# A hybrid transformer block on one core: two output heads projected together in the second feed-forward, its layernorm's last pass on ScalarE, and the first layernorms two tiles ahead

## The chip, the core and the metric

The kernel runs on one core of one Trainium2 chip. A core has a matrix engine (TensorE, "PE" in the profile, with its weight loads shown apart as "PEld"), a vector engine (VectorE, "DVE"), an engine for activations (ScalarE, "ACT"), a general engine (GpSimd, "POOL") and a synchronizing engine (SyncE, "SP"), which here only issues transfers. Each engine works through its own instructions in order; semaphores make one engine wait for another. Data lies in SBUF, 128 partitions wide; matrix products land in PSUM.

The metric is the device time of one execution in microseconds. Before the change it is 1683.34 us in the median of three runs (1683.14 to 1686.43).

## What is computed

The reference is a block of four residual stages over T = 1024 tokens of C = 512 channels, all in fp32:

```python
x = x + attn_a(layernorm(x), wq, wk, wv, wo)          # 32 heads of 16 channels, causal, rotary
x = x + ffn(layernorm(x), W_base, b_base, W_router, lora_A, lora_B)
x = x + attn_b(layernorm(x), Wq, Wk, Wv, Wo, ...)     # 32 heads of 128, 8 groups of keys and values, alibi
x = x + ffn(layernorm(x), W_base, b_base, W_router, lora_A, lora_B)

def layernorm(x):
    m = mean(x); v = var(x)
    return (x - m) / sqrt(v + eps)

def ffn(x, W_base, b_base, W_router, lora_A, lora_B): # the top 2 of 8 experts, rank 16 each
    w = top2_weights(softmax(x @ W_router.T))
    h = einsum('td,erd->ter', x, lora_A)
    return x @ W_base.T + b_base + 2.0 * einsum('ter,eor,te->to', h, lora_B, w)
```

The output of attn_b is the concatenation of its 32 heads times Wo, so it is a sum over heads: each head's 128 channels are multiplied with their own 128 rows of Wo. Which heads are summed in PSUM and which are added to x in SBUF is free, but for rounding.

## The kernel before

**Tiles.** x stays in SBUF in fp32 as NT = 8 tiles, x[0] to x[7], of 128 tokens by 512 channels. TensorE contracts over partitions, so a normalized tile is transposed first: `channels` (L118) makes four 128x128 transposes into PSUM (`transpose4`, L99; tiles tp_...) and copies them back with ScalarE (L121).

**The order of work.** A scheduler places each instruction on its engine by the order in which the program issues it, with some freedom by what is ready; the first layernorms' statistics are pinned to program order (`in_order`). From then on each engine's order is fixed. Pools of buffers (`bufs=`) set when a buffer may be written again.

**Layernorm.** `normalized` (L102 to L116) has bn_stats (L106), its aggregation (L110), the addition of eps (L112), all on VectorE, then the power -1/2 on GpSimd (`rsqrt`, L93: a tensor_tensor with a tile of -0.5, tile rs), then the last pass (L115) on VectorE: (x - mean) * rs, 128x512.

**Attention a, projections.** `project_qk` (inside `project_a`, from L202) runs over the tiles. In turn i it issues the four products of q for tile i (L179), the layernorm of tile i + 1, then `rotate` for q (L185 on ScalarE, L189 and L190 on VectorE), the transposes of tile i + 1 (`columns`, tiles tp_a), then the products of k and their rotation, and then what turn i - 1 left to be turned into rows (tp_aq, tp_ak). From the second half on, attention's own steps stand between these turns; among them are maxima over score tiles (L319, L322) on VectorE. The normalized tiles xn_a share the tag "w" (4 buffers) with ScalarE's outputs in `rotate`. The tiles of x are loaded by SyncE; weights are loaded by ScalarE's and SyncE's queues, and from the middle of attention a on by GpSimd.

**Attention b.** It works in 8 groups g of four query heads (hh = 0 to 3). For each head and tile i, `softmax` (L785 to L803) issues the score products (L791, tiles s), on VectorE the scaling with the alibi bias (L793), the maximum (L797) and its negation with the slope (L798), on ScalarE the exponential with its sum (L800), on VectorE the reciprocal (L802), on GpSimd the scaling (L803). Two tiles later `finish` issues the transposes of the probabilities by VectorE (L818, L824) and, at the end of a head (in the last group at its half too), the products with the values (L835; tiles o, and or for the rest), copied or added into oT, one for each head (L860, L876).

Between these steps TensorE is given other work as filler: `fill` is a generator that issues one matmul at each `next`. `due` says how many units of it are to be issued after the n-th tile of a group. Into the filler go the next group's projections and `project_o` (L636 to L648): for each tile t it multiplies oT of several heads with their rows of Wo into one PSUM tile (L642, tiles wo) and then adds it to x[t] on VectorE (L647). In the last group, g = 7, there is no next group. There the filler is the former group's projection (32 units), then heads 0 and 1 together (16 units: two matmuls and one addition for each tile), then head 2 alone (8 units: one matmul and one addition for each tile). Head 3 alone (8 more) is returned to the caller as `rest`, and runs in the second feed-forward. A tile's name has the group, the first head and the tile: wo7_2_4 is head 2's (and whatever is summed with it) product for tile 4. The wo tiles of the attention loop take turns in two PSUM buffers, those of the feed-forward in four.

**Feed-forward.** `ffn` (from L504) runs over NT + lag + 1 turns. In turn i it takes one turn of `before` (in the second feed-forward: the units of `rest`), `rows(i)` (the layernorm of tile i, xn_f with four buffers, then x[i] += bias on GpSimd, L525, which must come behind the last reading of x by the layernorm), `router(i - lag - 1)` (products with the router's and the experts' first weights, L534, tiles pr_f, copied by ScalarE, L535), `back(i - NT)` (products with W_base, L599, and with the second expert weights, added to x, L601) and `columns(i - lag)` (tp_f). After each four tiles comes `route`: a row of some thirty short VectorE instructions (L555 to L584) that picks two experts and ends in g_f; TensorE then transposes g_f (tp_g_f). The lag is 1 in the first feed-forward, f1, and 2 in the second, f2. Feed-forward f1 takes attention a's last output projections as its `before`; f2 ends with the transfers of the output, by SyncE.

Of the kernel before, what the change touches and what calls it, by code (L numbers as in the profile page):

```python
# [9 lines left out]
F32 = mybir.dt.float32  # L10
BF16 = mybir.dt.bfloat16
AF = mybir.ActivationFunctionType
ALU = mybir.AluOpType
# [3 lines left out]
P = 128  # L17
T = 1024
NT = T // P
C = 512  # L20
# [15 lines left out]
HKV = 8  # L36
GRP = HB // HKV
# [27 lines left out]
class Block:  # L65
# [33 lines left out]
            self.nc.tensor.transpose(ps[:, j, :], s, self.ident)  # L99
        return ps  # L100

    def normalized(self, i, xn, name, in_order=False):  # L102

        nc, sm = self.nc, self.sm
        st = sm.tile([P, 6], F32, tag="ln_st", name=f"st_{name}{i}")
        stats = nc.vector.bn_stats(st, self.x[i])  # L106
        if in_order:
            self.tc.keep_in_program_order(stats)
        mv = sm.tile([P, 2], F32, tag="ln_mv", name=f"mv_{name}{i}")
        nc.vector.bn_aggr(mv, st)  # L110
        ve = sm.tile([P, 1], F32, tag="ln_ve", name=f"ve_{name}{i}")
        nc.vector.tensor_scalar_add(ve, mv[:, 1:2], LN_EPS)  # L112
        rs = sm.tile([P, 1], F32, tag="ln_rs", name=f"rs_{name}{i}")
        self.rsqrt(rs, ve, [1])
        nc.vector.tensor_scalar(xn, self.x[i], mv[:, 0:1], rs, ALU.subtract, ALU.mult)  # L115
        return xn  # L116

    def channels(self, xn, dst, tp, name, tag="tp"):  # L118
# [31 lines left out]
    def project_a(self, ap, pt, work, ps_s, xnTs, qT, kT, v_p, wqT, wkT, wvT, rot):  # L150

        nc = self.nc

        w = {}

        def load(n, src, queue):
            w[n] = pt.tile([P, KC, C], F32, tag="p", name=f"w{n}")
            queue.dma_start(w[n], src.rearrange("(k p) n -> p k n", p=P))

        load("q", wqT, nc.scalar)  # L160
        rt = ap.tile([P, 4, NT], F32, tag="rot", name="rot_sb")
        nc.sync.dma_start(rt, rot)
        load("k", wkT, nc.sync)
        for i in range(2, NT):
            self.load_x(i)
        load("v", wvT, nc.sync)
        for n in range(6):
            self.transpose4(ps_s, [self.ident] * 4, f"i{n}", tag="s")
        rows = {}
        for n, fill in (("q", 0.0), ("k", 1.0)):  # L170
            t = pt.tile([P, 2, HA, PADA], F32, tag="p", name=f"r{n}")
            nc.gpsimd.memset(t[:, :, :, DA : DA + 1], fill)
            nc.gpsimd.memset(t[:, :, :, DA + 1 : PADA], 0.0)
            rows[n] = [t[:, a] for a in range(2)]

        def project(i, n):
            ps = ps_s.tile([P, C], F32, tag="s", name=f"pj_{n}{i}")
            for kc in range(KC):
                nc.tensor.matmul(ps, lhsT=xnTs[i][:, kc, :], rhs=w[n][:, kc, :], start=(kc == 0), stop=(kc == KC - 1))  # L179
            return ps  # L180

        def rotate(i, n, r, ps):
            cos, sin = rt[:, r, i : i + 1], rt[:, r + 1, i : i + 1]
            xs = work.tile([P, C], F32, tag="w", name=f"xs_{n}{i}")
            nc.scalar.activation(xs, ps, AF.Copy, scale=sin)  # L185
            pv = ps.rearrange("p (h d two) -> p h d two", d=DA // 2, two=2)
            sv = xs.rearrange("p (h d two) -> p h d two", d=DA // 2, two=2)
            dv = rows[n][i % 2][:, :, :DA].rearrange("p h (d two) -> p h d two", two=2)
            nc.vector.scalar_tensor_tensor(dv[:, :, :, 0], pv[:, :, :, 0], cos, sv[:, :, :, 1], ALU.mult, ALU.subtract)  # L189
            nc.vector.scalar_tensor_tensor(dv[:, :, :, 1], pv[:, :, :, 1], cos, sv[:, :, :, 0], ALU.mult, ALU.add)  # L190

        def to_rows(i, n, dst):

            for c0 in range(0, NCA, 4):
                src = [rows[n][i % 2][:, (c0 + c) * 4 : (c0 + c + 1) * 4, :].rearrange("p h d -> p (h d)") for c in range(4)]
                ps = self.transpose4(ps_s, src, f"a{n}{i}_{c0}", tag="s")
                copy = nc.scalar.copy if c0 else nc.vector.tensor_copy
                copy(dst[:, c0 : c0 + 4, i * P : (i + 1) * P], ps)

        pending = []  # L200

        def project_qk():  # L202
            def layernorm(i):
                return self.normalized(i, work.tile([P, C], F32, tag="w", name=f"xn_a{i}"), "a", in_order=True)

            def columns(i, xn):
                self.channels(xn, xnTs[i], ps_s, f"a{i}", tag="s")

            columns(0, layernorm(0))
            for i in range(NT):  # L210
                ps = project(i, "q")
                xn = layernorm(i + 1) if i + 1 < NT else None
                rotate(i, "q", 2, ps)
                if i + 1 < NT:
                    columns(i + 1, xn)
                rotate(i, "k", 0, project(i, "k"))
                while pending:
                    to_rows(*pending.pop(0))
                pending.extend([(i, "q", qT), (i, "k", kT)])
                yield  # L220

        def project_v():
            for i in range(NT):
                ps = project(i, "v")
                while pending:
                    to_rows(*pending.pop(0))
                nc.scalar.copy(v_p[:, i, :HA, :DA], ps.rearrange("p (h d) -> p h d", d=DA))
                yield

        return project_qk(), project_v()  # L230
# [273 lines left out]
    def ffn(self, name, before, after, lag):  # L504
# [4 lines left out]
        nc, tc, w = self.nc, self.tc, self.ffn_w  # L509
        H = NT // 2  # L510
        with ExitStack() as ctx:
            work = ctx.enter_context(tc.tile_pool(name=f"{name}_w", bufs=4))
# [4 lines left out]
            ps_m = ctx.enter_context(tc.tile_pool(name=f"{name}_pm", bufs=4, space=PSUM))  # L517
            xns, xnTs, lrs, gs, gTs = {}, {}, {}, {}, {}
# [1 line left out]
                lrs[half] = rp.tile([P, H, E + ER], F32, tag="lr", name=f"lr_{name}{half}")  # L520

            def rows(i):
                xns[i] = self.normalized(i, work.tile([P, C], F32, tag="xn", name=f"xn_{name}{i}"), name)

                nc.gpsimd.tensor_tensor(self.x[i], self.x[i], w["b"], ALU.add)  # L525

# [96 lines left out]
    def attention_b(self, ctx, wo_pool, WqT, WkT, WvT, WoT, qw, kw, xnT, missing, ffn_weights):  # L623
# [4 lines left out]
        nc, tc, sm = self.nc, self.tc, self.sm  # L628
# [5 lines left out]
        work = ctx.enter_context(tc.tile_pool(name="b_x", bufs=2))  # L634
# [15 lines left out]
        with ExitStack() as ctx:  # L650
# [227 lines left out]
            def in_turn(*gens):  # L878
                for g in gens:
                    yield from g  # L880
# [26 lines left out]
            for g in range(HKV):  # L907


                last = g == HKV - 1  # L910
                parts = []
                if not last:
                    wq, wkv = load_qkv(g + 1)
                    parts.append(project_kv(g + 1, wkv))
                    parts.append(project_q(g + 1, wq))
                if g:
                    parts.insert(-1, project_o(g - 1, wo, heads, ps_m, "m"))
                fill = in_turn(*parts)
                units = 74 if g else 42
                done = 0  # L920
                for hh in range(GRP):
                    if g and hh == 2:
                        if last:
                            for _ in fill:
                                pass
                        wo = load_o(g)
                        if last:
                            fill = in_turn(project_o(g, wo, [0, 1], ps_m, "m"), project_o(g, wo, [2], ps_m, "m"))
                    for i in range(NT):
                        p = softmax(g, hh, i)  # L930
                        n = hh * NT + i + 1
                        if not last:
                            due = units * n // (GRP * NT)
                        elif hh < 2:
                            due = max(0, (n - 2) * 32 // 14)
                        else:
                            due = 32 + max(0, 2 * (n - 19)) if n < 27 else 48 + (n - 27)
                        while done < due:
                            next(fill, None)
                            done += 1  # L940
                        pending.append((g, hh, i, p))
                        if len(pending) > LAG:
                            finish(*pending.pop(0))
                    if last and hh == GRP - 1:
                        for item in pending:
                            next(fill, None)
                            finish(*item)
                for _ in fill:
                    pass
                if g == HKV - 2:  # L950

                    self.load_ffn(wp, nc.sync, ("wkv", "wq"), *ffn_weights)
        return lambda ps_m: project_o(HKV - 1, wo, [GRP - 1], ps_m, "pm")


@with_exitstack
# [152 lines left out]
```

## Time and profile before

The profiled execution took 1683.11 us, of which the traced span is 1681.3 us. The page's first part gives each engine's busy time; the kernel's largest groups by TensorE are the score products of attention b (L791, 294.8 us), its query projections (L745, 246.2), and its output projection (L642, 241.8 us in 512 records: a product of 128x512 in fp32 appears as two records).

| quantity | value |
|---|---|
| median of the runs | 1683.34 us |
| profiled execution | 1683.11 us |
| its span | 1681.3 us |
| granted TensorE clock | 1.00 in every stretch looked at |
| L647 on VectorE, addition of a projected tile to x | 80 times, mean 677 ns |
| L115 on VectorE, last pass of the layernorm, xn_f | 16 times, mean 668 ns, median 546, longest 1561 |
| L93 on GpSimd, power for one tile's layernorm, rs_f | 16 times, mean 557 ns |
| L525 on GpSimd, addition of the bias to x | 16 times, mean 1306 ns |
| L121 on ScalarE, copy of a transposed tile, xnT_f | 16 times, mean 585 ns |

How to read such a page: busy times are summed over the span; a wait is an engine's idle time just before an instruction, with the instruction on another engine whose end released it. Idle time of an engine that is not the bottleneck costs nothing. A wait for several things is put down to what came last.

### The profile page before, as it was taken

Reading aid. Unit: us, or ns where it says so; the run is one execution under the profiler, and the core shown is the slowest. Engines: PE = TensorE matmul, PEld = TensorE weight load, DVE = VectorE, ACT = ScalarE, POOL = GpSimd, SP = SyncE. Lnnn points to the kernel's source line nnn. Section 1 sums busy time; section 2 is a strip of 40 time slices with the busy share of each in tenths; the row PEclk is TensorE's granted clock in tenths of the full one; section 3 lists DMA queues with packets and bytes.
Section 4 is the critical chain, followed back from the end, with each engine's and each line's share of the span. In section 5 each row is a group of like instructions: output and inputs, shape, how many; then the busy total and the mean of one; then the engine's idle time right before and its main releaser. Section 6 shows DMA issues by size and latency. Waiting matters only on the chain.

```text
span 1681.3 us, 32166 instructions
## 1 busy us (share of the span) xinstructions
PE 1652.6 (98%) x13016; PEld 940.7 (56%) x13016; DVE 1103.0 (66%) x2856; ACT 542.1 (32%) x1217; POOL 347.8 (21%) x508
## 2 busy tenths in 40 slices
PE   9999999999999999999999999999999999999988
PEld 5544444344555667556655665756655665566654
DVE  3556666662653886776677667676677766776773
ACT  2315555555111332233233223223223322322220
POOL 2000000000312332222123212222222321221140
PEclk9999999999999999999999999999999999999999
DMA  5000000001003201100200200110020020000001
GB/s 195 1 1 2 2 2 2 2 2 38 2 24 88 65 2 41 49 26 26 64 26 26 61 30 1 51 38 26 26 64 26 26 71 26 1 27 27 2 1 50
DMA packets 60868, 52.06 MB, mean 31 GB/s; under 512 B 5744, under 2 KB 47472, under 8 KB 60720
## 3 DMA queue, kind: packets, MB, share of 16 engines
q1 hardware_dynamic: 59408, 46.06, 9.2%
q0 software_dynamic: 784, 2.90, 0.4%
q8 instruction: 102, 1.67, 0.4%
q10 hardware_dynamic: 528, 1.05, 0.2%
q14 instruction: 46, 0.38, 0.1%
HBM read 30.98 MB, written 2.10 MB: 20 GB/s over the span
## 4 chain that ended last, share of the span: by engine, by line
PE 87%; DVE 10%; ACT 1%; POOL 1%; issue 1%; DVEq 0%; ACTq 0%; POOLq 0%
PE o L835 13%; PE pq L745 12%; PE s L791 12%; PE wo L642 9%; PE sT L354 7%; PE kv L700 7%; PE oT L389 5%; PE s L302 4%; PE pm_f L599 3%; PE or L835 3%; DVE p L793 3%; DVE nm L797 2%; DVE pT L818 2%; PE pj_v L179 2%; PE pm_ao L993 2%; PE pj_k L179 2%
## 5 line engine op out<-in xcount | busy, mean ns | idle before, releaser
L803 POOL TENSOR_SCALAR p<-p,rs 128x128 f32<-128x128 f32 (+7 forms) x256 | 190.8, 747 | 750.6 <-DVE rs L802 685.7
L800 ACT ACTIVATE p<-p,nm 128x128 f32<-128x128 f32 (+7 forms) x256 | 198.1, 774 | 453.4 <-DVE nm L798 443.0
L793 DVE SCALAR_TENSOR_TENSOR p<-s,rq,rel 128x512 f32<-128x512 f32 (+3 forms) x384 | 227.1, 605 | 119.4 <-PE s L791 118.8
L791 PE MATMUL s<-kT,qT 128*128 128x512 f32 (+3 forms) x768 | 294.8, 492 | 1.8 <-DVE p L793 1.5
L745 PE MATMUL pq<-xnTb,wq 128*128 128x512 f32 x512 | 246.2, 599 | 0.0
L642 PE MATMUL wo<-wo,oT 128*128 128x512 f32 x512 | 241.8, 594 | 3.4 <-DVE x L647 1.9
L791 PEld LDWEIGHTS s<-kT,qT 128*128 128x128 f32 x768 | 141.2, 190 | 165.8 <-issue 126.1
L835 PEld LDWEIGHTS o<-pT,va 32*128 32x128 f32 x5632 | 215.7, 185 | 28.5 <-DVE rs L802 11.8
L835 PE MATMUL o<-pT,va 32*128 32x128 f32 (+7 forms) x5632 | 224.6, 313 | 0.8
L818 DVE STREAM_TRANSPOSE pT<-p 128x640 f32<-128x640 f32 (+4 forms) x256 | 172.1, 673 | 73.1 <-PE o L835 54.7
L374 ACT ACTIVATE p<-sT 128x512 f32<-128x512 f32 (+1 forms) x320 | 157.5, 555 | 113.4 <-PE sT L372 70.9
L797 DVE TENSOR_REDUCE nm<-p 128x1 f32<-128x128 f32 (+7 forms) x256 | 188.2, 736 | 3.6
L302 PE MATMUL s<-kT,qT 32*128 32x512 f32 (+3 forms) x768 | 181.9, 522 | 0.0
L354 PE MATMUL sT<-qT,kT 32*128 32x512 f32 (+3 forms) x768 | 155.7, 521 | 0.0
L642 PEld LDWEIGHTS wo<-wo,oT 128*128 128x128 f32 x512 | 93.8, 190 | 87.5 <-issue 72.4
L745 PEld LDWEIGHTS pq<-xnTb,wq 128*128 128x128 f32 x512 | 92.3, 190 | 87.9 <-issue 80.2
L700 PE MATMUL kv<-wkv,xnTb 128*128 128x256 f32 x512 | 116.7, 382 | 4.4 <-DVE nm L798 4.0
L700 PEld LDWEIGHTS kv<-wkv,xnTb 128*128 128x128 f32 x512 | 95.8, 190 | 26.2 <-DVE nm L798 6.9
L319 DVE TENSOR_REDUCE part<-s 128x1 f32<-128x512 f32 x128 | 80.8, 684 | 40.6 <-PE s L302 36.0
L354 PEld LDWEIGHTS sT<-qT,kT 32*128 32x128 f32 x768 | 60.5, 183 | 62.2 <-issue 24.0
L860 ACT COPY oT<-o 128x1024 f32<-128x1024 f32 (+1 forms) x36 | 33.0, 916 | 181.8 <-PE o L835 176.6
L302 PEld LDWEIGHTS s<-kT,qT 32*128 32x128 f32 x768 | 76.4, 183 | 25.7 <-ACT p L374 10.3
(153 smaller groups left out, 1610.4 us busy)
## 6 DMA issues: line engine op xcount, KB each, us to landing
va<-v SPq DMA_DIRECT2D x256, 64.0 KB
wq<-in_b_WqT_dram SPq DMA_DIRECT2D x8, 1024.0 KB
wo<-in_b_WoT_dram SPq DMA_DIRECT2D x8, 1024.0 KB
x<-in_x_dram SPq DMA_DIRECT2D x8, 256.0 KB
wkv<-in_b_WkT_dram SPq DMA_DIRECT2D x8, 256.0 KB
wkv<-in_b_WvT_dram SPq DMA_DIRECT2D x8, 256.0 KB
out_dram<-x SPq DMA_DIRECT2D x8, 256.0 KB
wq<-in_a_wqT_dram ACTq DMA_DIRECT2D x1, 1024.0 KB
```

The source lines that it names most:

```text
L302: nc.tensor.matmul(made[j][:, at:end], lhsT=qT[rows_of(j), c, i * P : (i + 1) * P], rhs=kT[rows_of(j), c, kc * QC : kc * QC + end - at], s ...
L354: nc.tensor.matmul(made[j][:, at:end], lhsT=kT[rows_of(j), c, b * P : (b + 1) * P], rhs=qT[rows_of(j), c, (qc + 1) * QC - (end - at) : (qc ...
L642: nc.tensor.matmul(ps, lhsT=oTs[g, h][:, t * P : (t + 1) * P], rhs=wo[:, h, :], start=(h == heads[0]), stop=(h == heads[-1]))
L700: nc.tensor.matmul(ps.rearrange("p a b -> p (a b)"), lhsT=xnT[:, kc, i * P : (i + 1) * P], rhs=wkv[:, kc].rearrange("p a b -> p (a b)"), s ...
L745: nc.tensor.matmul(ps, lhsT=wq[:, kc, hh * DB : (hh + 1) * DB], rhs=xnT[:, kc, cols], start=(kc == 0), stop=(kc == KC - 1))
L791: nc.tensor.matmul(s, lhsT=qT[:, i * P : (i + 1) * P], rhs=kT[:, lo:hi], start=True, stop=True)
L793: nc.vector.scalar_tensor_tensor(p[:, lo:hi], s, rq[:, i : i + 1], rel[:, at + lo : at + hi], ALU.mult, ALU.add)
L797: nc.vector.tensor_reduce(nm, p[:, :w], AX.X, ALU.max, negate=True)
L800: nc.scalar.activation(p[:, :w], p[:, :w], AF.Exp, bias=nm, scale=slope, accum_out=ss)
L803: nc.gpsimd.tensor_scalar(p[:, :w], p[:, :w], rs, 1.0, ALU.mult, ALU.mult)
L818: nc.vector.transpose(PT[:, i : i + (NT - 1) * (m - 1) + 1 : NT - 1, :], p[:, : m * P].rearrange("p (j k) -> p j k", k=P))
L835: nc.tensor.matmul(cols(o[:, a], j), lhsT=vs[g][rows, j * NB + b, :], rhs=moving(j, rows, slice(b * B, (b + 1) * B)), start=(j == js[0] an ...
```

## The change

The change has three parts.

1. In `project_qk`, the layernorm of tile 1 is issued ahead of the loop, and turn i issues the layernorm of tile i + 2 instead of i + 1. The normalized tiles get a tag of their own with three buffers.
2. `normalized` gets a switch `scalar`, which the feed-forwards (both of them, as they share the code) set. With it, GpSimd computes mb = -(mean * rs) for the tile, 128x1, and ScalarE makes the last pass as Identity(rs * x + mb), in place of VectorE's subtract and multiply.
3. In the last group of attention b only heads 0 and 1 are projected in the attention loop, by a different `due`. Heads 2 and 3 are projected together in the second feed-forward, two matmuls and one addition for each tile, in place of one matmul and one addition there and one of each in the attention loop.

```diff
@@ normalized
-    def normalized(self, i, xn, name, in_order=False):
+    def normalized(self, i, xn, name, in_order=False, scalar=False):
...
         self.rsqrt(rs, ve, [1])
-        nc.vector.tensor_scalar(xn, self.x[i], mv[:, 0:1], rs, ALU.subtract, ALU.mult)
+        if scalar:
+            mb = sm.tile([P, 1], F32, tag="ln_mb", name=f"mb_{name}{i}")
+            nc.gpsimd.tensor_scalar(mb, mv[:, 0:1], rs, -1.0, ALU.mult, ALU.mult)
+            nc.scalar.activation(xn, self.x[i], AF.Identity, bias=mb, scale=rs)
+        else:
+            nc.vector.tensor_scalar(xn, self.x[i], mv[:, 0:1], rs, ALU.subtract, ALU.mult)
         return xn
@@ project_qk
             def layernorm(i):
-                return self.normalized(i, work.tile([P, C], F32, tag="w", name=f"xn_a{i}"), "a", in_order=True)
+                return self.normalized(i, work.tile([P, C], F32, tag="xn", name=f"xn_a{i}", bufs=3), "a", in_order=True)
...
             columns(0, layernorm(0))
+            xn = layernorm(1)
             for i in range(NT):
                 ps = project(i, "q")
-                xn = layernorm(i + 1) if i + 1 < NT else None
+                nxt = layernorm(i + 2) if i + 2 < NT else None
                 rotate(i, "q", 2, ps)
                 if i + 1 < NT:
                     columns(i + 1, xn)
+                xn = nxt
                 rotate(i, "k", 0, project(i, "k"))
@@ ffn, rows
-                xns[i] = self.normalized(i, work.tile([P, C], F32, tag="xn", name=f"xn_{name}{i}"), name)
+                xns[i] = self.normalized(i, work.tile([P, C], F32, tag="xn", name=f"xn_{name}{i}"), name, scalar=True)
@@ attention_b
                         if last:
-                            fill = in_turn(project_o(g, wo, [0, 1], ps_m, "m"), project_o(g, wo, [2], ps_m, "m"))
+                            fill = project_o(g, wo, heads[:2], ps_m, "m")
...
                         else:
-                            due = 32 + max(0, 2 * (n - 19)) if n < 27 else 48 + (n - 27)
+                            due = 32 + max(0, 16 * (n - 19) // 13)
...
-        return lambda ps_m: project_o(HKV - 1, wo, [GRP - 1], ps_m, "pm")
+
+        def remaining(ps_m):
+            units = project_o(HKV - 1, wo, heads[2:], ps_m, "pm")
+            for _ in range(NT):
+                for _ in heads[2:]:
+                    next(units)
+                yield
+
+        return remaining
```

## The prediction

> **What bounds the kernel now.** I read the page first (busy shares, the chain that ended last), then TensorE's waits, then busy time by stretch, then the timelines of the two stretches in which TensorE waits.
>
> ```profile
> span 1681.3 us, 32166 instructions
> ...
> PE 1652.6 (98%) x13016; PEld 940.7 (56%) x13016; DVE 1103.0 (66%) x2856; ACT 542.1 (32%) x1217; POOL 347.8 (21%) x508
> ...
> PE 87%; DVE 10%; ACT 1%; POOL 1%; issue 1%; DVEq 0%; ACTq 0%; POOLq 0%
> ```
>
> TensorE is busy for all but 1681.3 - 1652.6 = 28.7 us, and the change removes no matmul. So it can gain only out of these 28.7 us. Who owns them (line and tile, releaser, total, times, longest):
>
> ```profile
> PE kv L700 <- DVE nm L798: 4.0, 5, 0.8
> PE wo L642 <- DVE x L647: 1.9, 2, 1.3
> PE tp_a L99 <- DVE xn_a L115: 1.8, 2, 1.4
> PE tp_g_f L99 <- DVE g_f L584: 1.8, 1, 1.8
> PE pr_f L534 <- ACT xnT_f L121: 1.7, 1, 1.7
> PE tp_f L99 <- DVE xn_f L115: 1.7, 1, 1.7
> ```
>
> All but the first are places that the diff touches. By stretch (length, then busy time of PE, PEld, DVE, ACT, POOL): the first feed-forward, the end of attention_b, and the second feed-forward up to its first tp_g:
>
> ```profile
> 418.00:490.00 72.00, 70.84 (x273) 39.70 (x272) 44.45 (x130) 9.81 (x23) 19.16 (x26) 1.00 0.02 6
> ...
> 1557.00:1620.30 63.30, 59.81 (x867) 37.80 (x863) 47.84 (x103) 13.49 (x28) 11.42 (x15) 1.00 0.01 2
> 1620.30:1642.20 21.90, 16.71 (x94) 11.31 (x91) 18.40 (x53) 5.17 (x13) 13.23 (x13) 1.00 0.00 0
> ```
>
> TensorE idles 1.2, 3.5 and 5.2 us there, and DVE is busy for 84% of the last one. From tp_g at 1642.21 on, it works nearly without a gap. The granted clock is 1.00 throughout.
>
> **First layernorms two tiles ahead.** TensorE's two waits here:
>
> ```profile
> 19.41 0.66 PE L99 MATMUL tp_a<-ident,xn_a 128*128 128x128 f32 x4 [0.49 <-DVE xn_a L115]
> ...
> 67.53 0.63 PE L99 MATMUL tp_a<-ident,xn_a 128*128 128x128 f32 x4 [1.35 <-DVE xn_a L115]
> ```
>
> The second arises because four maxima of L322 (62.56 to 65.09) stand ahead of the seventh tile's layernorm on DVE. A tile earlier, that layernorm stands before them. Nothing is added: the same eight layernorms, with three buffers of their own; the bn_stats order is pinned. The risk is a new wait: the layernorm now stands a tile earlier than its x may have landed, ahead of rotate on DVE, with its pow ahead of DMA issues on POOL (10 to 13.5 us). Tile 2's bn_stats ran at 17.04 with no DMA wait; were x there only then, rotate's DVE part would end near 21.3, and tp_aq, its user, starts after 22.9. No transfer is moved on SP's queue. Bounds: -1.84 if both go, +0.5 if tile 2's x lands late. I take **-1.8**, since both waits have the row as their only releaser.
>
> **ScalarE's last pass.** Per tile and feed-forward it removes one DVE pass (xn_f, 546 ns undisturbed) and adds a 128x1 POOL multiply (mb) and a 128x512 Identity on ACT. Neither is in the trace. For ACT, the same shape with a bias pointer (L800) takes 719 ns, with a scale pointer (L185) 688. *ScalarE: Activation LUTs*, "What ACT_TABLE_LOAD costs", gives 186 ns + 0.833 per element + 93 per pointer operand: 186 + 427 + 2 x 93 = 0.80 us with two pointers; I take the row, 0.72, and keep 0.80. That page's "Rules for kernel authors" speaks against the edit: add and multiply belong on VectorE. By undisturbed rows it is right: 0.72 against 0.55. But beside POOL's L525 the DVE pass stretches (max 1561 ns), and DVE, not ACT (5.2 of 21.9 us busy), is crowded. For mb: POOL's tensor_scalar is 374 ns at 128 columns, 693 at 512, so a line through both gives 0.27 at one column; the 128x1 pow (L93) at 0.557 is the other end. I take 0.3.
>
> In the first feed-forward, xn_f is ready some 2 us before TensorE wants it (430.35 against 433.53), at the tightest tile 1 us (453.01 against 454.03); a path longer by 0.3 + 0.2 stays under this. The one wait there, 0.9 us, has the residual x as its other input. **0**, bounds -0.1 and +0.5 (the cover gone on one tile).
>
> **Heads 2 and 3 together.** Removed: eight adds at L647. Moved: head 2's eight matmuls (two records of 0.43, so 0.86 us each, 6.9 in all). Before, eight stand in the attention loop as fill; in the changed program's order, six fewer wo matmuls stand ahead of or_3, attention's last product (21 instead of 27), and eleven instead of five behind it. So TensorE's work up to or_3 shrinks by 6 x 0.86 = 5.2 us. Whether or_3 comes that much sooner depends on DVE's softmax chain, which ends there:
>
> ```profile
> 1601.87 1.09 DVE L797 TENSOR_REDUCE nm<-p 128x1 f32<-128x896 f32 x1
> 1602.87 0.68 DVE L647 TENSOR_TENSOR x<-x,wo 128x512 f32<-128x512 f32 x1
> 1603.47 0.15 DVE L798 TENSOR_SCALAR nm<-nm 128x1 f32<-128x1 f32 x1
> 1603.53 1.40 DVE L793 SCALAR_TENSOR_TENSOR p<-s,rq,rel 128x512 f32<-128x512 f32 x2
> 1604.88 0.16 DVE L802 RECIPROCAL rs<-ss 128x1 f32<-128x1 f32 x1
> 1604.96 0.67 DVE L647 TENSOR_TENSOR x<-x,wo 128x512 f32<-128x512 f32 x1
> 1605.54 1.21 DVE L797 TENSOR_REDUCE nm<-p 128x1 f32<-128x1024 f32 x1
> ```
>
> The adds sit between a maximum and its negation, so each delays the chain by its spacing of 0.60. In this stretch (1590 to 1610) eight stand; the changed order leaves four: 2.4 us off the chain. The last scores also come 5.2 us sooner, as six fill matmuls fewer stand ahead of them. Replayed by hand with the durations above, TensorE's waits before or_3 sum to about what they are now (0.3 to 0.7 before scores and product; 2.2 at wo_2_0, which takes the PSUM buffer that the add of tile 7 frees, where 1.3 was paid for wo_3_0; behind it stand three more wo and then the last product, which waits for DVE's chain anyway). **or_3 ends 5.2 us sooner**; bounds 2.4 (the adds alone) and 6.9 (all moved matmuls).
>
> Behind or_3, TensorE has 6 x 0.86 = 5.2 us more, of which 1.7 is met by two base matmuls (L599) that now stand behind tp_g instead of ahead of it. Per tile it has 2 x 0.86 (wo) + 0.93 (pr) + 0.44 (tp) = 3.09 us. The tile's feed through POOL, in order, is pow 0.55, mb 0.3, ACT's pass 0.72 (POOL's bias add L525 waits for it), L525 1.27, and gaps of some 0.25: 3.1 us. So POOL just keeps pace, and its idle in front of TensorE shrinks from 5.2 to about 1.3: 0.4 at pr of tile 5, 0.9 at tp_g, where DVE's 20 short instructions of route still stand. What waits behind ACT's Identity is xnT's copy (L121) and lr's (L535), 0.6 and 0.27 us, both short of their users. After tp_g all as before.
>
> So per term: end moves by (idle behind or_3) - (idle before, 5.2) + 5.2 of work - (lead of or_3), the base matmuls cancelling: 1.3 - 5.2 + 5.2 - 5.2 = **-3.9**. Sum: -1.8 + 0 - 3.9 = -5.7; I take 0.2 back for POOL's narrow margin: -5.5. The profiled execution took 1683.11 (span 1681.3 and 1.8 around it), the median is 1683.34: 1677.6 by the former, **1677.9** by the latter.
>
> **Rivals.** With I for the idle behind or_3 and L for its lead, each case is I - L - 1.84.
> A, the tail is a wash: the wait at wo_2_0 and those for scores grow to eat the fill that left, so L = 2.4, and I = 2.4: -1.8, **1681.5**. For it: the waits of this stretch are already there with the fill (3.5 us). Against: the scores themselves come sooner.
> B, all fits: I = 0, L = 6: -7.8, **1675.5**. Against: wo_2_0's wait and tp_g's are in the order.
> C, slower: POOL becomes the second feed-forward's bound. It serves pow, mb, then stands until ACT has passed, then adds; mb at 0.557, ACT at 0.80, and L525 drawn out beside DVE give 0.557 + 0.557 + 0.80 + 1.45 + 0.3 = 3.7 a tile, and ACT's pass held behind a copy that waits for TensorE adds 0.5: 4.2, which is 1.1 over TensorE's 3.09; six tiles of it make I = 6.6 + 0.9 = 7.5, and with L = 2.4 the change costs 7.5 - 2.4 - 1.84 = +3.3: **1686.6**. It decides from I = L + 1.84 on. For it: GpSimd's row is 13.2 busy of 21.9 us before mb is added, and *GPSIMD Engine Reference*, "1. Specifications", says that GpSimd shares its SBUF interfaces with VectorE. The trace agrees: L561 took 1.06 us beside L525, 0.19 elsewhere. At 0.19 for each such row the cost is nothing, at 1.06 some 0.9 on route's path. Against: the change takes DVE's passes and adds out of just this stretch.
> That the change doesn't do what it says is excluded by the order of instructions for heads and passes.
>
> **How the numbers follow.** Forecast (L 4 to 6, I 0.8 to 2.5) 0.62; A 0.18; B 0.09; C 0.11. The range, 1675.0 to 1682.8, holds forecast, B and most of A, and leaves C and the edges out; the likeliest alone is 1676.5 to 1680. About what a measurement can tell from none is 0.2%, 3.4 us: faster below 1680.0 takes the forecast, B and a little of A, 0.72; nearly all of A and a third of C within, 0.20; the rest, 0.08, slower.
>
> **What would show it.** Right: no wait tp_a on xn_a (-1.8); or_3's end some 5 us sooner counted from the last group's first score; no waits of 1.7 for tp_f and pr_f in the second feed-forward; tp_g's below 1.2; ACT's Identity 0.70 to 0.80, POOL's mb near 0.3. Wrong: tp_f waiting for ACT's xn tile after tile, with POOL's L525 closely spaced above 3.1 us (C); wo_2_0 or the scores waiting over 4 us (A); a DMA wait ahead of the third layernorm; mb above 0.56.

## The result, and the profile after

Five runs of the changed kernel took 1678.20 us in the median (1677.98 to 1678.67), against 1683.34 before; the ratio is 0.9965, with a 95% interval of 0.9953 to 0.9977. The profiled execution took 1678.20 us, its span 1676.2: 5.1 us less than before's.

The page after (span; busy time of each engine):

```profile
span 1676.2 us, 32185 instructions
...
PE 1653.2 (99%) x13016; PEld 941.1 (56%) x13016; DVE 1089.3 (65%) x2832; ACT 554.0 (33%) x1233; POOL 350.7 (21%) x524
```

TensorE's idle time fell from 28.7 to 1676.2 - 1653.2 = 23.0 us. Its waits after, of the tiles that the change touches (releaser, total, times, longest; line numbers have moved on by up to 16):

```profile
PE wo L650 <- DVE nm L806: 2.6, 2, 1.8
PE tp_g_f L99 <- DVE g_f L592: 2.0, 2, 1.1
...
PE pr_f L542 <- ACT xnT_f L127: 0.6, 1, 0.6
```

The waits of tp_a, and of tp_f for xn_f, are gone; pr_f's has shrunk from 1.7 to 0.6; tp_g's is as long as it was, 2.0 against 1.8. Points that both timelines of TensorE have in common take the 5.1 us apart (or_1 and or_3 are the groups of products with the values, tiles or, of heads 1 and 3 of the last group; or_3 is attention's last product):

| stretch | before, us | after, us | difference |
|---|---|---|---|
| start to the first kv product of attention b | 495.39 | 493.10 | -2.29 |
| to the start of or_1 | 1058.93 | 1058.67 | -0.26 |
| start of or_1 to the end of or_3 | 65.97 | 58.63 | -7.34 |
| end of or_3 to the first instruction behind the first tp_g | 22.60 | 23.46 | +0.86 |
| to the end of the span | 38.41 | 42.34 | +3.93 |

The last row is the surprise. The changed order puts two base products there that stood ahead of tp_g, 1.72 us; 2.2 us more have no work to account for them. TensorE's timeline after, around tp_g (start, duration, in brackets the idle time before and its releaser), and then its clock there, microsecond by microsecond (window; length; busy time of PE, PEld, DVE, ACT, POOL; granted clock; DMA share; GB/s):

```profile
1628.90 1.19 PE L542 MATMUL pr_f<-w_small,xnT_f 128*128 128x136 f32 x8 [0.59 <-ACT xnT_f L127]
1629.93 1.02 PE L607 MATMUL pm_f<-w_base,xnT_f 128*128 128x512 f32 x2
1632.10 0.30 PE L99 MATMUL tp_g_f<-ident,g_f 128*128 128x128 f32 x1 [1.15 <-DVE g_f L592]
1633.29 0.73 PE L99 MATMUL tp_g_f<-ident,g_f 128*128 128x128 f32 x3 [0.89 <-DVE g_f L592]
1633.86 3.25 PE L607 MATMUL pm_f<-w_base,xnT_f 128*128 128x512 f32 x4
```

```profile
1633.00:1634.00 1.00, 0.71 (x4) 0.58 (x5) 0.64 (x3) 0.00 (x0) 0.09 (x1) 1.00 0.00 0
1634.00:1635.00 1.00, 1.00 (x3) 0.39 (x2) 0.69 (x1) 0.00 (x0) 0.00 (x0) 0.61 0.00 0
1635.00:1636.00 1.00, 1.00 (x2) 0.34 (x1) 0.00 (x0) 0.00 (x0) 0.00 (x0) 0.50 0.06 16
1636.00:1637.00 1.00, 1.00 (x3) 0.43 (x2) 0.00 (x0) 0.00 (x0) 0.00 (x0) 0.50 0.00 0
1637.00:1638.00 1.00, 1.00 (x3) 0.39 (x2) 0.00 (x0) 0.00 (x0) 0.00 (x0) 0.68 0.00 0
```

Four records of 128x512 take 3.25 us where they take 1.88 at full clock: the granted clock is 0.50. Summed over the windows it lacks 0.39 + 0.50 + 0.50 + 0.32 = 1.71 us of full speed. The last transfer accounts for another 0.43: from the start of VectorE's last addition to the end of the span it is 3.99 us before and 4.42 after. This is not the change's: in the traces it is either 3.9 to 4.0 or about 4.4, and 3.92 in a kernel with the same second feed-forward (ScalarE's pass in it alone, below). What decides it stays open.

### The profile page after: what moved, and what is told of

Same layout as the page of the kernel before. It is cut to its first block, busy times and chain, and to the rows that moved or that the text cites. A ratio compares the mean times of both kernels' runs of the same rounds, so it can differ in the third digit from the quotient of the medians.

```text
span 1676.2 us, 32185 instructions
## 1 busy us (share of the span) xinstructions
PE 1653.2 (99%) x13016; PEld 941.1 (56%) x13016; DVE 1089.3 (65%) x2832; ACT 554.0 (33%) x1233; POOL 350.7 (21%) x524
## 4 chain that ended last, share of the span: by engine, by line
PE 87%; DVE 10%; POOL 1%; ACT 1%; issue 0%; ACTq 0%; DVEq 0%; POOLq 0%
PE o L843 13%; PE s L799 12%; PE pq L753 12%; PE wo L650 9%; PE sT L362 7%; PE kv L708 7%; PE oT L397 5%; PE s L310 4%; PE pm_f L607 3%; PE or L843 3%; DVE p L801 3%; DVE nm L805 2%; DVE pT L826 2%; PE pj_v L185 2%; PE pj_q L185 2%; PE pj_k L185 2%
```

## The experiments

Each kernel ran beside the kernel before on one chip; ratios are to before, with their 95% intervals. The median of before was 1684.4 us in the series of the four first experiments and 1683.5 to 1683.6 in the others, so the ratios compare better than the medians. Theory and rival were these: the gain comes from three places whose sizes the prediction gave (first layernorms 1.8, lead of or_3 5.2, idle behind it 1.3); or it sits in one part and another part takes from it.

**The parts alone.** First, the layernorms alone.

```diff
-                xn = layernorm(i + 1) if i + 1 < NT else None
+                nxt = layernorm(i + 2) if i + 2 < NT else None
```

> Only the first layernorms two tiles ahead. Theory (the two waits of tp_a for xn_a, 0.49 and 1.35 us, sit on TensorE's path and nothing takes their place): 1.8 to 2.4 us faster than before, about 1681.3; both waits gone, the first tp_f of the first feed-forward 1.8 to 2.4 us earlier, the tail unchanged. Rival (TensorE would have waited a little later anyway): under 0.7 us.

The ratio was 0.9989 (0.9983 to 0.9996), so 1.9 us; the median 1682.45. The waits of 0.49 and 1.35 us were gone, and nothing took their place later on. One new wait of 0.2 us for xn_a stood at the very first tile: in other executions of kernels with and without this part it varied from 0 to 1.1, at the start, where tile 0 is awaited. As expected.

Second, ScalarE's pass alone.

```diff
+            nc.gpsimd.tensor_scalar(mb, mv[:, 0:1], rs, -1.0, ALU.mult, ALU.mult)
+            nc.scalar.activation(xn, self.x[i], AF.Identity, bias=mb, scale=rs)
```

> Only the last pass of the feed-forwards' layernorms on ScalarE. Theory (with one wo matmul per tile TensorE has 2.2 us of work a tile, and the chain pow, mb, ACT's pass, bias add on GpSimd is some 3.2 to 3.4 a tile, so the feed takes VectorE's place as the limit): within 1 us of before, 1682.5 to 1684.5, with tp_f waiting for ACT's xn. Rival (VectorE's crowding alone made the waits of 1.67 and 1.71 us): 3.4 us faster, 1680.

The ratio was 1.0001 (0.9993 to 1.0010): alone no gain shows. Its waits show why (same columns as above):

```profile
PE pr_f L539 <- ACT xnT_f L126: 2.6, 2, 2.2
...
PE tp_g_f L99 <- DVE g_f L589: 1.0, 1, 1.0
...
PE tp_f L99 <- ACT xn_f L118: 0.6, 1, 0.6
```

tp_f's and pr_f's 3.4 us have become 3.2, all of it now behind ScalarE, and only tp_g's wait is 0.8 shorter. The theory held in the time; tp_f waits for ScalarE's pass for only 0.6, and 2.6 stand at pr_f, behind the copy of the transposed tile. The rival, that VectorE's crowding alone made these waits, fell.

Third, the heads alone.

```diff
-                            fill = in_turn(project_o(g, wo, [0, 1], ps_m, "m"), project_o(g, wo, [2], ps_m, "m"))
+                            fill = project_o(g, wo, heads[:2], ps_m, "m")
```

> Only heads 2 and 3 together in the second feed-forward. Theory (the gain comes from the end of attention, the moved matmuls cover the second feed-forward's waits whichever engine makes the last pass): or_3 ends some 7 us sooner behind or_1 than before, and 2.5 to 3.5 us of it are left at the end, 1680 to 1681. Rival (without ScalarE's pass VectorE's waits of 1.7 us for tp_f and pr_f stay): no more than 1 us faster.

The ratio was 0.9985 (0.9978 to 0.9991), 2.5 us, the median 1681.52. From or_1's start to or_3's end it took 58.64 us, the changed kernel's 58.63 within a hundredth: the whole lead is this part's. But behind it tp_g waited for twice as long, and the clock was granted at 0.5 from 1636 to 1643:

```profile
1637.55 1.08 PE L99 MATMUL tp_g_f<-ident,g_f 128*128 128x128 f32 x4 [3.98 <-DVE g_f L584]
```

So the rival was right that VectorE's load matters, and wrong in where: tp_f and pr_f no longer wait (two wo matmuls a tile cover them), tp_g does. That asked for the changed kernel without ScalarE's pass (the second edit taken back):

> The changed kernel without ScalarE's pass (VectorE keeps the last pass of the feed-forwards' layernorms). Theory (with the heads' matmuls behind it TensorE reaches tp_g sooner than VectorE, which still has the passes among route's instructions): tp_g waits near 4.0 us and the clock is granted at 0.5 behind it for twice as long, so it is 1 to 2 us slower than the changed kernel, a ratio to before of 0.997 to 0.998. Rival (ScalarE's pass is worth as little as it is alone): 0.9965, within 0.5 us of the changed kernel.

The wait of 4.0 us was there, as expected, but TensorE did a base product more ahead of it, pr_f did not wait, and the clock lay at 0.5 for 3.4 us, as long as in the changed kernel and not twice as long. The time was only 0.9970 (0.9959 to 0.9981), against 0.9965 and 0.9967 for the changed kernel in two series: no difference that these intervals show. The theory had the wait and missed its price. By the medians (1678.62 against 1678.20 and 1678.54) ScalarE's pass adds under half a microsecond to the other two parts; whether it adds anything is not settled.

**What made or_3 come sooner.** Before, with head 2's additions in the last group left out, and its matmuls kept.

```diff
-                nc.vector.tensor_add(self.x[t], self.x[t], ps)
+                if heads != [2]:
+                    nc.vector.tensor_add(self.x[t], self.x[t], ps)
```

> Before, with the eight additions of head 2's product in the last group left out, and its matmuls kept (so head 2 of the last group is missing from the output). Theory (the additions lie on VectorE's chain at the end of attention, 0.60 us each, seven of them in the stretch where TensorE waits): or_3 ends 3 to 4.5 us sooner, and most of it is left at the end, 1679 to 1681. Rival (the fill that went is the cause of the lead, the additions sat in gaps): under 1.5 us.

The ratio was 0.9981 (0.9973 to 0.9988), the median 1680.87: the theory held, the rival fell. The stretch from or_1's start to or_3's end, in this kernel, before and in the changed one (one view of each, columns as above):

```profile
1553.99:1616.41 62.42, 62.31 (x958) 41.10 (x957) 45.42 (x100) 13.62 (x28) 11.97 (x16) 1.00 0.01 2
```

```profile
1554.32:1620.29 65.97, 62.48 (x956) 40.47 (x955) 48.12 (x104) 13.49 (x28) 11.42 (x15) 1.00 0.01 2
```

```profile
1551.77:1610.40 58.63, 56.87 (x944) 38.20 (x943) 40.97 (x92) 13.61 (x28) 11.38 (x16) 1.00 0.01 2
```

Without the additions TensorE idles for 62.42 - 62.31 = 0.1 us instead of 65.97 - 62.48 = 3.5, and or_3 ends 3.6 us sooner although one wo matmul more stands ahead of it. So nearly all of TensorE's idling there came from these additions, but not by the softmax chain alone. The two longer waits of wo before, and the one that the changed kernel has left:

```profile
1605.68 1.12 PE L642 MATMUL wo<-wo,oT 128*128 128x512 f32 x2 [0.61 <-DVE x L647]
...
1609.86 1.96 PE L642 MATMUL wo<-wo,oT 128*128 128x512 f32 x4 [1.33 <-DVE x L647]
```

```profile
1598.17 3.70 PE L650 MATMUL wo<-wo,oT 128*128 128x512 f32 x8 [1.76 <-DVE nm L806]
```

With another wait of 0.60, put down to a negation directly behind an addition, wo stands for 2.5 of the 3.5 us behind an addition that has yet to read the PSUM buffer it needs; only 0.28 + 0.67 are scores that wait for VectorE's scaling. Leaving the additions out removes both, so the chain's delay and the wait for a buffer are not told apart. The changed kernel has 5.6 us less work in this stretch and idles for 1.8, at one place: wo_2_0, behind the last addition of heads 0 and 1 (the trace names nm, which stands directly behind that addition and ends 0.05 us later; in the heads alone the same wait, 1.77, is put down to the addition).

**Tp_g's wait and the clock.** First, the base products of tile 0 ahead of tp_g.

```diff
                     if i == NT:
+                        base(0)
                         weighted(0)
```

Here `base(i)` issues the four products with W_base that `back(i)` began with.

> The changed kernel, with all four base products of tile 0 (L607) issued ahead of tp_g in the second feed-forward instead of two. Theory (TensorE waits 1.15 + 0.89 us around tp_g, and because it does little in those 3 us its clock is then granted at 0.5 for some 3.7 us, which costs 1.7 us): two matmuls, 1.7 us, fill the wait, the clock stays at 1.00, and it ends 2.5 to 3.8 us sooner than the changed kernel, a ratio to before near 0.9945. Rival 1 (the dip has nothing to do with the wait): 1.7 us sooner, clock still 0.5 behind tp_g. Rival 2 (the moved work only changes places): within 0.5 us of the changed kernel.

The ratio was 0.9948 (0.9935 to 0.9960), the median 1675.22, 3.0 us less than the changed kernel's. Around tp_g 0.5 us of waiting was left, and the clock behind it was 1.00. The theory held; rival 1, that the dip has nothing to do with the wait, fell: it foresaw a gain of 1.7 us. One trace with the clock at 1.00 could be chance, as the next experiment shows, but the ten runs with these products ahead (five here, five below) lie between 1674.72 and 1675.96. Next, GpSimd's bias addition moved away from the layernorm:

```diff
             def rows(i):
...
-                nc.gpsimd.tensor_tensor(self.x[i], self.x[i], w["b"], ALU.add)
...
+                nc.gpsimd.tensor_tensor(self.x[i], self.x[i], w["b"], ALU.add)
                 nc.vector.tensor_add(self.x[i], self.x[i], ps)
```

> The changed kernel, with GpSimd's bias addition issued behind the last product of its tile instead of directly behind the layernorm, in both feed-forwards. Theory (the bias addition beside VectorE stretches route's instructions: L564 0.99 us for 0.19, the four of g_f 1.97 for 0.89): tp_g's wait of 2.0 us shrinks below 0.5, the clock dip behind it goes, 2.5 to 3.5 us sooner than the changed kernel. Rival (route is late because its inputs are): within 0.7 us of it.

> Both of the above: base products ahead of tp_g and the bias addition late. Theory: TensorE has no wait of over 0.5 us between or_3 and the end, and the clock stays at 1.00; 3 to 4 us sooner than the changed kernel, about 0.9943 of before; little better than either alone, since both remove the same 3.7 us. Rival: no better than the changed kernel.

Neither tried what it was meant to: the scheduler put the addition where it had been, and each engine's order was, instruction for instruction, the changed kernel's and the former experiment's. So they are repeats: 0.9967 (0.9954 to 0.9979) and 0.9949 (0.9936 to 0.9963). The first is useful for that. Two of its five runs took 1677.1 us, the others 1678.6 to 1679.8, and in its profiled execution, one of the two, TensorE waited at tp_g for the same 1.14 and 0.89 us, and its clock stayed at 1.00:

```profile
1632.00:1634.00 2.00, 0.40 (x2) 0.24 (x2) 1.93 (x6) 0.52 (x2) 1.26 (x1) 1.00 0.00 0
1634.00:1636.00 2.00, 2.00 (x7) 1.11 (x8) 0.94 (x3) 0.00 (x0) 0.00 (x0) 1.00 0.00 0
```

From behind tp_g to the end it took 40.63 us, 1.71 less than the 42.34 above: with the same instructions in the same order, just the clock. In the first feed-forward, the pass given back to VectorE:

```diff
-                xns[i] = self.normalized(i, work.tile([P, C], F32, tag="xn", name=f"xn_{name}{i}"), name, scalar=True)
+                xns[i] = self.normalized(i, work.tile([P, C], F32, tag="xn", name=f"xn_{name}{i}"), name, scalar=name == "f2")
```

> The changed kernel, with ScalarE's last pass in the second feed-forward alone (VectorE's again in the first). Theory (the first feed-forward has slack, the pass there is worth nothing): within 0.5 us of the changed kernel. Rival (it loses 0.2 us or more in the first): up to 1 us sooner.

The ratio was 0.9964 (0.9952 to 0.9977), the median 1678.15: in the first feed-forward the edit makes no difference that shows, as expected; the first kv product of attention b starts at 493.62, within the 492.99 to 493.90 of the kernels that have ScalarE's pass there. Then the changed kernel again, and the bias additions moved in earnest: in the second feed-forward they are pinned to program order behind the product's addition (tile 7's ahead of its own, behind tile 6's).

> The changed kernel once more, on the chip of the next two. Theory: TensorE waits 2.0 us in two pieces around the first tp_g, the granted clock falls to 0.5 behind it in most executions, and the time is 0.9965 of before, give or take 0.001. Rival (the dip was an accident of the first chip): clock 1.00 there, 1.3 us less.

```diff
+                if name == "f2" and i == NT - 1:
+                    tc.keep_in_program_order(nc.gpsimd.tensor_tensor(self.x[i], self.x[i], w["b"], ALU.add))
                 nc.vector.tensor_add(self.x[i], self.x[i], ps)
+                if name == "f2" and i < NT - 1:
+                    tc.keep_in_program_order(nc.gpsimd.tensor_tensor(self.x[i], self.x[i], w["b"], ALU.add))
```

> The changed kernel with, in the second feed-forward, GpSimd's bias additions behind the product's addition (tile 7's ahead of its own, behind tile 6's), so that none runs beside the first route; the orders of TensorE and VectorE are those of the changed kernel. Theory (route's instructions are stretched beside GpSimd: L564 0.99 us for 0.19, L577 0.47 for 0.19, the four of g_f 1.97 for 0.89): these fall to 0.19, 0.19 and 0.89, tp_g's wait of 2.0 us falls below 0.5, pr's of 0.6 goes, and with them the clock dip: 2.5 to 3.7 us sooner than the changed kernel. Rival (route's inputs are late, its stretched instructions don't matter): the rows are shorter, but the wait stays over 1.3 us and the time within 0.8 us of the changed kernel.

The changed kernel came out at 0.9967 (0.9955 to 0.9980), the clock again at 0.5 behind tp_g: the rival fell. With the additions moved it was 0.9939 (0.9927 to 0.9952), the median 1673.88 against 1678.54, 4.7 us less and more than expected. VectorE's instructions of route in the changed kernel, the three of GpSimd's beside them, and then the same three of VectorE's with the additions moved:

```profile
1624.99 1.27 POOL L533 TENSOR_TENSOR x<-x,w_small 128x512 f32<-128x512 f32 x1 [0.93 <-ACT xn_f L119]
...
1625.32 0.99 DVE L564 TENSOR_TENSOR sh_f<-lr_f,mx_f 128x32 f32<-128x32 f32 x1
...
1628.29 1.27 POOL L533 TENSOR_TENSOR x<-x,w_small 128x512 f32<-128x512 f32 x1 [0.93 <-ACT xn_f L119]
...
1629.14 0.47 DVE L577 TENSOR_TENSOR hot_f<-eq_f,fm_f 128x32 f32<-128x32 f32 x1
...
1631.67 1.97 DVE L592 TENSOR_TENSOR g_f<-lr_f,wt_f 128x128 f32<-128x128 f32 x4
1631.83 1.26 POOL L533 TENSOR_TENSOR x<-x,w_small 128x512 f32<-128x512 f32 x1 [0.93 <-ACT xn_f L119]
```

```profile
1625.46 0.16 DVE L565 TENSOR_TENSOR sh_f<-lr_f,mx_f 128x32 f32<-128x32 f32 x1
...
1628.48 0.18 DVE L578 TENSOR_TENSOR hot_f<-eq_f,fm_f 128x32 f32<-128x32 f32 x1
...
1630.76 0.90 DVE L593 TENSOR_TENSOR g_f<-lr_f,wt_f 128x128 f32<-128x128 f32 x4
```

0.99 for 0.16, 0.47 for 0.18, 1.97 for 0.90: 2.2 us of route were lost beside GpSimd, and the wait at tp_g was as long mainly for that reason: from L564's start to the end of g_f it takes 8.3 us in the one and 6.2 in the other. The edit also shortens GpSimd's work for each tile, and route starts 0.65 us sooner behind or_3. With the additions moved it is 0.2 us, pr_f's is gone, and the clock is 1.00. Of the 4.7 us, 1.8 are tp_g's wait, 0.6 pr_f's and 1.7 the clock; 0.4 are the last transfer, which varies as said above. Both remedies together:

> That, and the base products of tile 0 ahead of tp_g. Theory: no wait of TensorE above 0.3 us in the second feed-forward, clock 1.00, 0.5 to 1.2 us sooner than with the base products ahead alone (1675.2), the fastest of all: about 1674.3. Rival: the same as with the base products alone.

The ratio was 0.9935 (0.9921 to 0.9948), the median 1673.35. No wait of TensorE stands in the second feed-forward any more. It has the lowest time of all, 1.9 us below the base products alone (on another chip), where 0.5 to 1.2 was expected. Its interval lies below the changed kernel's (0.9955 to 0.9980), but overlaps both that of the base products alone and that of the bias additions alone, so the base products' share is not told apart there.

## Why the prediction was right, and where it was not

The time, 1677.9 against 1678.2, was right, and so was the place of each gain: the start, the end of attention and the idle time behind it. The terms behind it were less good: the start and the lead of or_3 came out 2.8 us better, what lies behind or_3 3.5 us worse. That they nearly cancel is luck.

**First layernorms, -1.8.** Right: alone 1.9 us, the two waits gone, tile 2's x not late. The 2.55 us of the profiled execution include scatter: the first kv product of attention b starts anywhere between 492.78 and 493.90 in the ten traces with this part, and between 495.17 and 496.08 in the four without; the means differ by 2.2.

**First feed-forward, 0.** Nothing speaks against it (0.9964 with the edit there taken back). In the prediction's first example 430.35 is where xn_f starts; it is ready at 430.90, so the slack is 2.6 us.

**ScalarE's pass.** The row chosen for its cost, 0.72 us from an activation with one pointer operand, was the wrong one: Identity with two took 0.813 us in the mean. The Trainium skill (*ScalarE: Activation LUTs*, "What ACT_TABLE_LOAD costs") had given 0.80 and was nearer. mb took 0.265 for the 0.3 assumed. In the feed of a tile these two errors and shorter gaps (some 0.17 for 0.25) nearly cancel, and it came out at the 3.1 us predicted: L533 started at 1618.86, 1621.92 and 1624.99. GpSimd thus just keeps TensorE's pace of 3.08, and rival C did not come about. Beside the other two parts the pass showed no gain of its own (0.9970 without it), so the prediction's sum is carried by the heads and the first layernorms.

**Lead of or_3, 5.2.** It was 7.3, above even the 6.9 given as its bound. The step that failed: "TensorE's waits before or_3 sum to about what they are now". They fell from 3.5 to 1.8, and 0.4 of TensorE's busy time went beside the six matmuls. The reading of the additions was off as well: of the eight between 1590 and 1610 only two (1602.87 and 1606.67) stand between a maximum and its negation, and two stand behind the last negation (1607.27). What they held up was for the larger part the next wo itself, which waited for their PSUM buffer; without them 0.1 us of idling is left.

**Idle behind or_3, 1.3.** It was 0.59 + 1.15 + 0.89 = 2.6, just outside the 0.8 to 2.5 of the forecast. pr_f's was 0.6 for 0.4; the term that was mis-sized is tp_g's, 0.9, for which 2.0 was measured. The prediction had the cause, GpSimd's bias addition beside route, in rival C with "at 1.06 some 0.9 on route's path", and left it out of the forecast's sum. Counted from or_3's end, g_f starts at 21.5 us before and at 21.3 after, but the last bias addition starts at 17.0 before and at 21.4 after, and so falls beside g_f, which it had not touched before (0.89 there). It comes as late (21.5) in the changed kernel without ScalarE's pass, and at 18.4 with that pass alone; so it is mainly TensorE's longer turn for each tile, with two wo products, that moved it, and not the longer feed through GpSimd.

**"After tp_g all as before."** This failed: 1.7 us went to a clock of 0.5, which the prediction did not consider, and 0.4 to the last transfer.

Against the predicted -5.5 the sum is: the start 0.7 better (2.55 for 1.84), the lead 2.1 better, the idle 1.3 worse, what lies behind tp_g 2.2 worse, the 0.2 taken back not needed: -5.0, which is the span's -5.1 but for rounding.

## What to carry to other kernels

An accumulation split by what is ready pays twice on the vector engine, and where the matrix engine waits for that engine an addition costs much of its length: eight of 0.67 us cost 3.6 us here, 0.44 each. Adding in PSUM what can wait for a later stage brought attention's end 7.3 us forward for 5.2 us of moved matmuls, but of that only 2.5 us were left at the end when the heads were moved alone. Work that is moved into a stage shifts what runs beside what in it: list which instructions of two engines will now overlap. And a wait of the matrix engine can cost more than its length, so work that can stand ahead of the wait belongs there.

## What the runs showed of the hardware

**The clock falls after a stretch of little work, not only of none, and not always.** In the changed kernel it fell to 0.50 at 1634.23, for 3.41 us, after three microseconds in which TensorE was busy for 1.0 (0.00, 0.30 and 0.71 in the windows from 1631 on). The Trainium skill (*TensorE: Matmul & The Clock Gate*, Part 1, "What's actually happening") describes a free-running window of 3.4 us, and half rate after an idle one; the length agrees, but TensorE was not idle. Why the same wait brought no fall in the repeat can be worked out from the traces. In the changed kernel the clock rose again at 1637.64 and fell once more, behind the last product, at 1675.19: the two falls are 40.96 us apart, 12 steps of 3.413. The repeat's only fall, also behind the last product, came at 1672.97; steps counted back from there end at 1632.01 and 1635.42. So the step with the wait in the changed kernel, and the one with the longer part of it in the repeat, are these (columns as above):

```profile
1630.82:1634.23 3.41, 1.37 (x6) 0.78 (x6) 2.85 (x9) 0.97 (x2) 1.34 (x2) 1.00 0.00 0
```

```profile
1632.01:1635.42 3.41, 1.81 (x7) 1.05 (x8) 2.87 (x7) 0.51 (x2) 1.26 (x1) 1.00 0.00 0
```

TensorE was busy for 1.37 of 3.41 us in the one and for 1.81 in the other. The other traces give steps of 0.62 (heads alone), 1.29 (without ScalarE's pass) and 1.66 (the pass in the second feed-forward alone) with a fall behind them, and of 1.54 (also without ScalarE's pass) and 1.64 (base products ahead, from 1595.91 on) without one. So the limit is, as an estimate from these, between 1.4 and 1.7 us of a step and not sharp in these records, and where the steps lie differs from execution to execution. The times of before have two levels that fit this, though its one trace shows no fall: of its 60 runs in the first series, the 16 with a mean granted clock of 1.000 have a median of 1683.2 us, and the 34 with 0.999 one of 1684.5. This mean also counts a fall behind the last product, which costs nothing.

**Some VectorE instructions stretch until GpSimd's ends, others do not.** A 128x32 TENSOR_TENSOR of 0.16 us took 0.99 beside a 128x512 addition on GpSimd; in the kernels that kept VectorE's pass, one of 0.19 took 1.26. Each ended some 0.05 us behind GpSimd's addition. All that were held so in route read two tiles in SBUF. A TENSOR_REDUCE of route (fm_f, at 1628.41 in the changed kernel, 0.18 us), a RECIPROCAL (before, 1637.33, 0.18) and an addition that reads one of its tiles from PSUM (L647 before, at 1627.94, 0.68) ran beside such an addition at their usual length. A share of busy time does not show this: it stood in the longest of a group's durations.
